# Softmax without the division: undivided probabilities, and weighted values multiplied by reciprocal sums that are spread over channels through memory

## The chip, the core and the metric

The kernel runs on one core of one Trainium2 chip. The metric is the device time of one execution in microseconds, the median over several runs. Names of engines: PE multiplies matrices (PEld are its weight loads), DVE is VectorE, ACT is ScalarE, POOL is GpSimd, SP is the engine that here only issues transfers (DMAs). PSUM is the memory into which PE writes, in 8 banks of 128 x 512 numbers.

## The reference, cut

Two layers over x of shape (8, 512, 256), all in 32-bit floats. Layer 1 (the code's L0) is attention with 16 heads of 64 channels, rotary embeddings and a causal mask, with a quantised linear map beside it; layer 2 (L1) is a masked softmax mixing with a small gated network beside it. The change touches layer 1's attention alone:

```python
xn = layernorm(x)
q, k = rope(xn @ Wq + bq), rope(xn @ Wk + bk)          # 16 heads of 64
v = xn @ Wv + bv
scores = einsum('bnqd,bnkd->bnqk', q, k) / 8           # causal: later keys get -1e9
attn = softmax(scores)                                  # exp(s - max) / sum
attended = einsum('bnqk,bnkd->bnqd', attn, v)           # concatenated over the heads
x = x + attended @ Wo + bo + quantised_linear(xn)
```

## The kernel before

**Units of work.** A step `at` of layer 1 is half of one batch element: 8 of its 16 heads, as four pairs j = 0..3. There are 16 steps, 0 to 15 (`last`); the prediction calls a step a "head" for short ("head 8" is the step at = 8). A step's queries are cut into 16 blocks of 32; block i has scores against its first 32(i+1) keys only. Partition j*32+q of a score tile holds query q of a block for pair j; the second axis e tells the two heads of a pair apart.

**A step, by function.**
- `project_qk(2*at + half, which)` multiplies on PE (tile `pq`, L428), evicts on ACT with a bias (`l`, L434), and sends four DMAs that swap 32-row blocks into a tile `y` (L436). `turn_own` (DVE, `h`, L446) and `turn_other` (DVE `y`, L446, then the sum `h + y` on POOL, L461) apply the rotation. `l` and `y` have two buffers each.
- `scores(at, run)` (PE, `sc`, L509) fills banks for one of five runs of blocks, `soften(at, run)` subtracts the maximum on DVE (L537) and takes the exponential on ACT with the row sums `sm` (L541).
- `divide(at, run)` takes reciprocals of the sums on DVE (L552) and multiplies every block of probabilities by them, on POOL (L560) or, in two places of step 0, on ACT (L558).
- `turn(at, run)` transposes the probabilities in 32 x 32 blocks on DVE (L580), as PE needs keys on the partitions.
- `project_v` and `load_v` bring v, through memory, into the tile `vr` (L472 to L489). `weigh(at)` multiplies it with the turned probabilities (PE, `av`, L597). `keep_weighed(at)` evicts the four results on ACT, adding v's bias as a bias per partition (L611).
- `finish(at)` is `output_product` (PE with `Wo`, `pw`, L390) and `add_output` (DVE, L399) into `x1s[b]`.

**The order** is written out by hand: instructions go to each engine's queue in program order and every engine runs its own queue in order, waiting on semaphores. In the loop over `at`, step at's scores are interleaved with `weigh(at - 1)`, the projections of steps at + 1 and at + 2, and `finish(at - 1)`:

```python
scores(at, 0)
turn(at - 1, 4)
soften(at, 0)
weigh(at - 1)
keep_weighed(at - 1)
turn_qk(2 * at + 2, 1)
load_v(at)
divide(at, 0)
turn_qk(2 * at + 3, 1)
```

Even steps also fetch x of the batch element (`fetch(b)`, 512 KB, L376). Even steps 4 to 12 also turn the next element's input by way of memory (`turn_x`: DVE `xs` L325, a DMA to `xnf` L329, four DMAs to `xnT` L188), which the projection at the end of the same step reads. `add_biases(b)` adds `bo` and another bias to `x1s[b]` on POOL. After step 15 layer 2 follows; its first pieces are already mixed into steps 14 and 15.

Of the kernel before, what the change touches and what calls it, by code (L numbers as in the profile page):

```python
# [8 lines left out]
F32 = mybir.dt.float32  # L9
BF16 = mybir.dt.bfloat16  # L10
I8 = mybir.dt.int8
AF = mybir.ActivationFunctionType
ALU = mybir.AluOpType
# [3 lines left out]
P = 128  # L17
B, S, D = 8, 512, 256
# [11 lines left out]
Q = 32  # L30
# [1 line left out]

UNITS = ((15,), (14, 0), (13, 1), (12, 2), (11, 3), (10, 4), (9, 5), (8, 6), (7,))
RUNS = (UNITS[0:2], UNITS[2:4], UNITS[4:6], UNITS[6:8], UNITS[8:9])
PLACE = {i: n for n, i in enumerate(i for us in UNITS for i in us)}


BIAS = 2 * S
# [6 lines left out]
def two_layers(  # L45
# [14 lines left out]
    def bank(name):  # L60
        return ps.tile([P, S], F32, tag="b", name=name)
# [198 lines left out]
    with ExitStack() as c0:  # L260
# [11 lines left out]
        def line(name):  # L272
            return work.tile([P, S], F32, tag="w", name=name, bufs=2)
# [104 lines left out]
        def add_biases(b):  # L378
            for t in range(NT):
                nc.gpsimd.tensor_tensor(x1s[b][:, t, :], x1s[b][:, t, :], bob, ALU.add)  # L380

        products = {}

        def output_product(at, half):
# [131 lines left out]
        def soften(at, run):  # L516

            if at not in sums_of:
                sums_of[at] = [
                    small.tile([P, 2 * len(PLACE)], F32, tag=f"{n}16", name=f"{n}_{at}", bufs=2)  # L520
                    for n in ("nm", "sm", "rs")
                ]
            nm, sm, _ = sums_of[at]
            for us in RUNS[run]:
                if (at, run) == (last, 0):
                    p = qk.tile([P, 2, S], F32, tag="h0", name=f"p_{at}_{us[0]}")
                elif (at, run) == (0, len(RUNS) - 1):
                    p = work.tile([P, 2, S], F32, tag="xnl", name=f"p_{at}_{us[0]}")
                else:
                    p = prob.tile([P, 2, S], F32, tag="p", name=f"p_{at}_{us[0]}")  # L530
                col = 0
                for i in us:
                    n = Q * (i + 1)
                    chances[at, i] = p[:, :, col : col + n]
                    for e, sc in enumerate(scored.pop((at, i))):
                        c = 2 * PLACE[i] + e
                        nc.vector.tensor_tensor_reduce(  # L537
                            p[:, e, col : col + n], sc, cmask[:, S - n :], -1.0 / L**0.5, BIG,
                            ALU.add, ALU.min, nm[:, c : c + 1],
                        )  # L540
                        nc.scalar.activation(  # L541
                            p[:, e, col : col + n], p[:, e, col : col + n], AF.Exp,
                            bias=nm[:, c : c + 1], scale=-1.0, accum_out=sm[:, c : c + 1],
                        )
                    col += n

        def divide(at, run, on_act=False):
            _, sm, rs = sums_of[at]
            for us in RUNS[run]:
                first = 2 * PLACE[us[0]]  # L550
                which = slice(first, first + 2 * len(us))
                nc.vector.reciprocal(rs[:, which], sm[:, which])  # L552
                for i in us:
                    for e in range(2):
                        c = 2 * PLACE[i] + e
                        p = chances[at, i][:, e, :]
                        if on_act and us is RUNS[run][-1]:
                            nc.scalar.activation(p, p, AF.Copy, scale=rs[:, c : c + 1])  # L558
                        else:
                            nc.gpsimd.tensor_scalar(p, p, rs[:, c : c + 1], 1.0, ALU.mult, ALU.mult)  # L560

        def pitch(c):
            return NT * 4 - 4 * c - 1
# [36 lines left out]
            weighed[at] = banks  # L603

        def keep_weighed(at):
            g = at % NH
            for j, av in enumerate(weighed.pop(at)):
                atts[at, j] = attp.tile([P, S], F32, tag="att", name=f"att_{at}_{j}")

                bv = BIAS + 2 * NP + 4 * g + j  # L610
                nc.scalar.activation(atts[at, j], av, AF.Identity, bias=cs[:, bv : bv + 1])  # L611

# [194 lines left out]
        scores(0, 1)  # L809
        project_qk(2, 0)  # L810
        soften(0, 1)
        divide(0, 0)
        turn_other(2, 1)
        turn_own(2, 0)
        greatest_of(1)
        turn(0, 0)
        divide(0, 1, on_act=True)
        turn_other(2, 0)
        project_qk(3, 1)
        load_v(0)  # L820
# [2 lines left out]
        soften(0, 2)  # L823
        transpose_x(1)
        turn_own(3, 1)
        divide(0, 2)
        turn_other(3, 1)
        turn(0, 1)
        scores(0, 3)
# [3 lines left out]
        soften(0, 4)  # L833
        project_v(1, (1,))
        turn_qk(3, 0)
        divide(0, 3, on_act=True)
        divide(0, 4)
        turn(0, 2)
        x_next.append(load_x(2))
        turn(0, 3)  # L840
# [1 line left out]
        for at in range(1, last):  # L842
            b, g = divmod(at, NH)
            two = at + 2 <= last
            if g == 0 and b < B - 1:
                fetch(b)
            scores(at, 0)
            turn(at - 1, 4)
            soften(at, 0)
            if at == last - 3:  # L850
                scale_of_x()
            weigh(at - 1)
            keep_weighed(at - 1)
            if at == 1:
                load_rest()
                load_second()
                fetch(0)
            turn_qk(2 * at + 2, 1)
            load_v(at)
            if at in (last - 3, last - 2):  # L860
                s_ = at - last + 3
                fetch_output(s_, output_tile(f"x1e_{s_}"))
                xnl = fetch_input(s_, work.tile([P, NK * S], F32, tag="xnl", name=f"xnl_{s_}"))
            divide(at, 0)
            turn_qk(2 * at + 3, 1)
            if at == last - 2:
                first_norm = norm(0, xpool.tile([P, NT, D], F32, tag="x", name="yn_0"))
            scores(at, 1)
            soften(at, 1)
            turn(at, 0)  # L870
            if at == 2:
                look_at(2)
            elif at == 4:
                spread_rest()
                spread_second()
            elif g == 1 and 1 <= b < B - 2:
                look_at(b + 2)
            divide(at, 1)
            if at == last - 1:
                first_norm()  # L880
            project(at + 1, 0)
            if at in (last - 3, last - 2):
                round_input(xnl)
            scores(at, 2)
            soften(at, 2)
            turn_qk(2 * at + 2, 0)
            turn(at, 1)
            if at in (last - 3, last - 2):
                xq = work.tile([P, NK * S], BF16, tag="xq", name=f"xq_{s_}")
                clip(xnl, xq)  # L890
            divide(at, 2)
            if at == 2:
                prepare(2)
            elif g == 1 and 1 <= b < B - 2:
                prepare(b + 2)
            if g == 0 and 1 < b < B - 1:
                turn_x(b + 1)
                if b + 2 < B:
                    x_next.append(load_x(b + 2))
            if at == last - 1:  # L900
                turn_qk(2 * at + 3, 0)
            if at == 1:
                nc.gpsimd.tensor_tensor(bob, bob, rw[:, 2, :], ALU.add)
                add_biases(0)
            project_v(at + 1)
            if at == last - 1:
                break
            if at == 2:
                transpose_x(2)
                x_next.append(load_x(3))  # L910
            scores(at, 3)
            soften(at, 3)
            turn_qk(2 * at + 3, 0)
            turn(at, 2)
            divide(at, 3)
            scores(at, 4)
            soften(at, 4)
            if at in (last - 3, last - 2):
                for half in range(2):
                    add_quantised(s_, half, xq, line(f"u_{s_}_{half}"))  # L920
            finish(at - 1)
            turn(at, 3)
            if two:
                project(at + 2, 1)
            divide(at, 4)
            if g == 0 and b < B - 1:
                add_biases(b)
            if at == last - 4:
                greatest()
# [4 lines left out]
        soften(at - 1, 3)  # L934
        nc.sync.dma_start(w2, second.rearrange("j (k p) n -> p j k n", p=P))
        turn(at - 1, 2)
        divide(at - 1, 3)
        scores(at - 1, 4)
        soften(at - 1, 4)
        output_product(at - 2, 0)  # L940
        scores(at, 0)
        soften(at, 0)
        add_output(at - 2, 0)
        divide(at - 1, 4)
        output_product(at - 2, 1)
        turn_input(0, whole("yt_0", S + 1))
        for s in (1, 0):
            mix_before(0, s)
        turn(at - 1, 3)
        turn(at - 1, 4)  # L950
        add_output(at - 2, 1)
        fetch(B - 1)
        divide(at, 0)
        scores(at, 1)
        soften(at, 1)
        weigh(at - 1)
        for s in (1, 0):
            mix_own(0, s)
        stats_1 = statistics(x1s[1], "b1")
        divide(at, 1)  # L960
        keep_weighed(at - 1)
        load_v(at)
        late[2] = fetch_input(2, work.tile([P, NK * S], F32, tag="xnl", name="xnl_2"))
# [3 lines left out]
        soften(at, 2)  # L967
        sides_of(0, first_sides[:, 0, :], first_sides[:, 1, :])
        turn(at, 1)
        divide(at, 2)  # L970
        scores(at, 3)
        soften(at, 3)
        for half in range(2):
            output_product(at - 1, half)
        turn(at, 2)
        divide(at, 3)
        for half in range(2):
            add_output(at - 1, half)
        scores(at, 4)
        soften(at, 4)  # L980
        turn(at, 3)
        divide(at, 4)
        kk = key(0)
        turn(at, 4)
        r = gate(0)
        round_late(2)
        weigh(at)
# [122 lines left out]
```

## Time and profile before

| what | value |
|---|---|
| three runs | 935.48, 935.68, 936.91 us |
| median | 935.68 us |
| profiled execution, first to last instruction (span) | 934.3 us |
| median less span | 1.4 us |
| TensorE clock granted | 1.000 throughout |
| PE busy, by the page | 919.8 us |
| POOL busy | 542.2 us, of which L560 265.4 us |
| DMA traffic | 108.03 MB, mean 116 GB/s |

The profile shows one execution; its own time outside the span is not given, so the median less the span stands for it. Lines of the profile begin with the start and the length in microseconds or with a source line; "idle before" is the time in which the engine had nothing to run just ahead of that piece, and the name after the arrow is what ended it, inferred from semaphores ("issue" where the profile shows nothing).

### The profile page before, as it was taken

How to read it: one execution, taken by the hardware profiler on the slowest of the kernel's cores; microseconds unless marked ns; L12 is line 12 of the kernel's file. 1: busy time of each engine (PE TensorE's matmuls, PEld its weight loads, DVE VectorE, ACT ScalarE, POOL GpSimd, SP SyncE). 2: the span in 40 equal slices, each digit the busy share in tenths (PEclk: the TensorE clock that was granted, in tenths of full speed). 3: DMA queues.
4: the chain of work that ended last, by engine and by line, in shares of the span. 5: the costliest groups of instructions: out<-in, count | busy, mean ns of one | idle time of the engine just before them, and what ended most of it. 6: DMA issues, size and time to landing. Idle time of an engine off the chain costs nothing.

```text
span 934.3 us, 27432 instructions
## 1 busy us (share of the span) xinstructions
PE 919.8 (98%) x10451; PEld 594.7 (64%) x10451; DVE 793.3 (85%) x2441; ACT 528.3 (57%) x1478; POOL 542.2 (58%) x688
## 2 busy tenths in 40 slices
PE   9998999999999999999999999999999999999998
PEld 5446565656566575757565656566657777777776
DVE  4998898898899889988998899999899588888854
ACT  3585564647465646474746556555577444445553
POOL 2576766655665667566665756678667323444311
PEclk9999999999999999999999999999999999999999
DMA  7667354525543464245444635563435133221011
GB/s 213 194 165 213 102 138 130 121 75 132 169 105 97 109 182 132 75 115 172 123 95 114 179 93 145 151 154 97 110 108 127 47 102 79 74 50 48 25 33 34
DMA packets 70290, 108.03 MB, mean 116 GB/s; under 512 B 8592, under 2 KB 49040, under 8 KB 70160
## 3 DMA queue, kind: packets, MB, share of 16 engines
q1 hardware_dynamic: 68288, 104.64, 42.2%
q10 hardware_dynamic: 1872, 1.64, 0.7%
q8 instruction: 83, 1.36, 0.6%
q14 instruction: 47, 0.39, 0.1%
HBM read 41.76 MB, written 28.84 MB: 76 GB/s over the span
## 4 chain that ended last, share of the span: by engine, by line
PE 85%; DVE 6%; DMA 3%; issue 1%; POOL 1%; SPq 1%; ACT 1%; DVEq 0%; ACTq 0%; POOLq 0%
PE pq L428 21%; PE av L597 14%; PE sc L509 11%; PE pw L390 10%; PE pv L472 8%; PE po L756 6%; PE pk L703 3%; PE pg L718 3%; PE pvv L730 3%; DVE t L580 2%; PE c L675 2%; PE trc L743 1%; PE plr L245 1%; DVE p L537 1%; DMA xnl<-xnf 1%
## 5 line engine op out<-in xcount | busy, mean ns | idle before, releaser
L541 ACT ACTIVATE p<-p,nm 128x64 f32<-128x64 f32 (+15 forms) x512 | 260.0, 512 | 123.8 <-DVE nm L537 100.9
L560 POOL TENSOR_SCALAR p<-p,rs 128x512 f32<-128x512 f32 (+4 forms) x504 | 265.4, 547 | 44.6 <-DVE rs L552 42.6
L461 POOL TENSOR_TENSOR h<-h,y 128x1024 f32<-128x1024 f32 x62 | 161.1, 2598 | 181.5 <-DVE y L446 102.2
L537 DVE CUSTOM_DVE_ANT_0 p<-sc,cmask 128x64 f32<-128x64 f32 (+15 forms) x512 | 190.2, 434 | 53.7 <-PE sc L509 53.7
L580 DVE STREAM_TRANSPOSE t<-p 128x256 f32<-128x256 f32 (+3 forms) x640 | 192.2, 367 | 17.9 <-POOL p L560 17.8
L509 PE MATMUL sc<-h,h 64*32 64x512 f32 (+15 forms) x4096 | 138.7, 393 | 1.3 <-POOL h L461 1.2
L597 PE MATMUL av<-t,vr 32*64 32x384 f32 (+15 forms) x4096 | 128.8, 392 | 3.7 <-issue 3.7
L597 PEld LDWEIGHTS av<-t,vr 32*64 32x64 f32 x4096 | 122.8, 131 | 9.2 <-issue 7.9
L509 PEld LDWEIGHTS sc<-h,h 64*32 64x32 f32 x4096 | 78.6, 106 | 78.5 <-issue 58.3
L434 ACT ACTIVATE l<-pq,cs 128x512 f32<-128x512 f32 x128 | 84.7, 683 | 67.6 <-PE pq L428 53.3
L390 PE MATMUL pw<-wo,att 128*128 128x256 f32 x512 | 114.9, 382 | 0.8 <-DVE nm L537 0.8
L446 DVE TENSOR_TENSOR y<-y,cs 128x1024 f32<-128x1024 f32 x64 | 110.6, 1728 | 5.1 <-DMA y<-l 5.1
L428 PE MATMUL pq<-xnT,wq 128*128 128x512 f32 x256 | 114.6, 599 | 0.2 <-ACT xnT L349 0.2
L428 PE MATMUL pq<-xnT,wk 128*128 128x512 f32 x256 | 113.1, 593 | 1.4 <-DVE x L399 1.0
L472 PE MATMUL pv<-wv,xnT 128*128 128x512 f32 x256 | 114.3, 599 | 0.0
L390 PEld LDWEIGHTS pw<-wo,att 128*128 128x128 f32 x512 | 95.9, 190 | 19.5 <-issue 6.1
L541 ACT ACTIVATION_READ_ACCUMULATOR p<-p,nm 128x1 f32 x512 | 97.3, 190 | 0.0
L428 PEld LDWEIGHTS pq<-xnT,wk 128*128 128x128 f32 x256 | 48.3, 190 | 58.2 <-issue 55.4
L472 PEld LDWEIGHTS pv<-wv,xnT 128*128 128x128 f32 x256 | 47.3, 190 | 57.9 <-issue 54.5
L446 DVE TENSOR_TENSOR h<-l,cs 128x1024 f32<-128x1024 f32 x64 | 80.0, 1252 | 4.3 <-ACT l L434 4.3
L428 PEld LDWEIGHTS pq<-xnT,wq 128*128 128x128 f32 x256 | 47.2, 190 | 56.0 <-issue 48.8
L611 ACT ACTIVATE att<-av,cs 128x512 f32<-128x512 f32 x64 | 38.7, 688 | 71.3 <-PE av L597 71.3
(114 smaller groups left out, 940.7 us busy)
## 6 DMA issues: line engine op xcount, KB each, us to landing
y<-l SPq DMA_DIRECT2D x256, 128.0 KB, 2.3
va<-v SPq DMA_DIRECT2D x32, 512.0 KB, 3.1
vr<-va SPq DMA_DIRECT2D x64, 256.0 KB, 5.1
x<-in_x SPq DMA_DIRECT2D x15, 512.0 KB, 5.0
x1f<-x SPq DMA_DIRECT2D x7, 512.0 KB, 3.2
out<-y SPq DMA_DIRECT2D x14, 256.0 KB, 2.2
xnf<-xs SPq DMA_DIRECT2D x5, 512.0 KB, 3.6
xnT<-xnf SPq DMA_DIRECT2D x20, 128.0 KB, 2.8
```

Source lines behind the costliest of these rows:

```text
L390: nc.tensor.matmul(pw[:, j, :], atts[at, p][:, tok], wo[:, 4 * (at % NH) + p, :], start=(p == 0), stop=(p == 3),)
L428: nc.tensor.matmul(pb.rearrange("p (t a r) -> p t a r", a=4, r=Q), w[:, g, k, bass.ts(t, P)], xnT[b][:, k].rearrange("p a (t r) -> p t a r ...
L434: nc.scalar.activation(l[:, t, :], pb, AF.Identity, bias=cs[:, bias : bias + 1])
L446: nc.vector.tensor_tensor(dst, src, table[:, None, :].to_broadcast([P, 2, S]), ALU.mult)
L461: (engine or nc.gpsimd).tensor_tensor(h, h, y, ALU.add)
L472: nc.tensor.matmul(pb.rearrange("p (g n) -> p g n", g=2), xnT[b][:, k, 2 * half + j], wqkv[2][:, 2 * g : 2 * g + 2, k, :], start=(k == 0), ...
L509: nc.tensor.matmul(scored[at, i][e][j * Q : j * Q + Q, :], q[rows, j % 2, bass.ts(i, Q)], k[rows, j % 2, :n], start=True, stop=True,)
L537: nc.vector.tensor_tensor_reduce(p[:, e, col : col + n], sc, cmask[:, S - n :], -1.0 / L**0.5, BIG, ALU.add, ALU.min, nm[:, c : c + 1],)
L541: nc.scalar.activation(p[:, e, col : col + n], p[:, e, col : col + n], AF.Exp, bias=nm[:, c : c + 1], scale=-1.0, accum_out=sm[:, c : c + 1],)
L560: nc.gpsimd.tensor_scalar(p, p, rs[:, c : c + 1], 1.0, ALU.mult, ALU.mult)
L580: nc.vector.transpose(turned[at][c][:, :, at_ : at_ + (n - 1) * pitch(c) + 1 : pitch(c), :], p[:, :, c * P : c * P + n * Q].rearrange("p e ...
L597: nc.tensor.matmul(banks[j][e * L : e * L + L, i * Q :], vs[at][rows, c, m, bass.ts(e, L)], t[c][rows, e, m * pitch(c) + m : m * pitch(c) ...
```

## The change

Probabilities stay undivided: `divide` and its calls are gone. The sums of step at get columns by head and block (e*16 + i). A new function `settle(at)`, called after the last `turn(at, ..)`, takes all reciprocals at once, transposes them on DVE, writes them to memory (16 KB) so that they lie in the order of queries, and reads them back twice, once for each head of the pairs, repeated over the 64 partitions that are that head's channels. `keep_weighed` copies the results of `weigh` on ACT and multiplies them with that tile on POOL (in step 15 two of the four are multiplied on DVE, from PSUM). As v's bias can no longer be added there, `gather_bias` (step 1) and `spread_bias` (step 2) multiply it with `Wo` once and add it to `bob`, the bias that `add_biases` adds; the first `add_biases` moves from step 1 to step 2. A setting of the program's scratch for DMA descriptors is made smaller.

```diff
+        def gather_bias():
+            both = line("bvwo").rearrange("p (j n) -> p j n", j=2)
+            ones = line("ones")[:, :P]
+            nc.gpsimd.memset(ones, 1.0)
+            for p in range(NP):
+                bv = BIAS + 2 * NP + p
+                nc.gpsimd.tensor_scalar(
+                    both[:, min(p, 1), :], wo[:, p, :], cs[:, bv : bv + 1], None, ALU.mult
+                )
+                if p:
+                    nc.gpsimd.tensor_tensor(both[:, 0, :], both[:, 0, :], both[:, 1, :], ALU.add)
+            nc.gpsimd.tensor_tensor(bob, bob, rw[:, 2, :], ALU.add)
+            gathered[0] = ones, both[:, 0, :]
+
+        def spread_bias():
+            pb = bank("bvwo")
+            nc.tensor.matmul(pb[:, :D], *gathered.pop(0), start=True, stop=True)
+            nc.vector.tensor_tensor(bob, pb[:, :D], bob, ALU.add)
...
-                        c = 2 * PLACE[i] + e
+                        c = e * (S // Q) + i
...
-        def divide(at, run, on_act=False):
-            _, sm, rs = sums_of[at]
-            for us in RUNS[run]:
-                first = 2 * PLACE[us[0]]
-                which = slice(first, first + 2 * len(us))
-                nc.vector.reciprocal(rs[:, which], sm[:, which])
-                for i in us:
-                    for e in range(2):
-                        c = 2 * PLACE[i] + e
-                        p = chances[at, i][:, e, :]
-                        if on_act and us is RUNS[run][-1]:
-                            nc.scalar.activation(p, p, AF.Copy, scale=rs[:, c : c + 1])
-                        else:
-                            nc.gpsimd.tensor_scalar(p, p, rs[:, c : c + 1], 1.0, ALU.mult, ALU.mult)
+        def settle(at):
+            sm = sums_of.pop(at)[1]
+            rs = small.tile([P, Q], F32, tag="rs16", name=f"rs_{at}", bufs=2)
+            turned_ = small.tile([P, Q], F32, tag="rt16", name=f"rt_{at}", bufs=2)
+            nc.vector.reciprocal(rs, sm)
+            nc.vector.transpose(turned_, rs)
+            there = away.tile([4, 2, S], F32, tag="rs", name=f"rsf_{at}")
+            nc.sync.dma_start(there.rearrange("j e (i q) -> (j e i) q", q=Q), turned_)
+            shares[at] = work.tile([P, 4, S], F32, tag="share", name=f"share_{at}")
+            for e in range(2):
+                nc.sync.dma_start(
+                    shares[at][e * L : e * L + L], there[:, e, :][None].to_broadcast([L, 4, S])
+                )
...
-                bv = BIAS + 2 * NP + 4 * g + j
-                nc.scalar.activation(atts[at, j], av, AF.Identity, bias=cs[:, bv : bv + 1])
+                if at == last and j % 2:
+                    nc.vector.tensor_tensor(atts[at, j], av, shares[at][:, j, :], ALU.mult)
+                else:
+                    nc.scalar.copy(atts[at, j], av)
+                    nc.gpsimd.tensor_tensor(atts[at, j], atts[at, j], shares[at][:, j, :], ALU.mult)
...
             scores(at, 0)
             turn(at - 1, 4)
+            settle(at - 1)
             soften(at, 0)
...
-            divide(at, 0)
             turn_qk(2 * at + 3, 1)
...
             if at == 1:
-                nc.gpsimd.tensor_tensor(bob, bob, rw[:, 2, :], ALU.add)
+                gather_bias()
+            elif at == 2:
+                spread_bias()
                 add_biases(0)
...
-    nc = bacc.Bacc("TRN2", target_bir_lowering=False, num_devices=1)
+    nc = bacc.Bacc(
+        "TRN2", target_bir_lowering=False, num_devices=1, dynamic_dma_scratch_size=1024
+    )
```

The other calls of `divide` (those of step 0, of the loop and of the end written out for steps 14 and 15) are deleted in the same way; in that end `settle(at - 1)` follows `turn(at - 1, 4)`, and `settle(at)` follows the last `turn(at, 4)`.

## The prediction

> **What bounds the kernel now.** I read the engine shares first, then PE's own timeline for its gaps, then the rows of the work that the change touches, then one head's transfers in order.
>
> The engine line, the clock line and the chain's summary by engine, from the page:
>
> ```profile
> PE 919.8 (98%) x10451; PEld 594.7 (64%) x10451; DVE 793.3 (85%) x2441; ACT 528.3 (57%) x1478; POOL 542.2 (58%) x688
> PEclk9999999999999999999999999999999999999999
> PE 85%; DVE 6%; DMA 3%; issue 1%; POOL 1%; SPq 1%; ACT 1%; DVEq 0%; ACTq 0%; POOLq 0%
> ```
>
> PE is busy for 98% at full clock. From one `av` to the next (165.17 to 209.41, 255.54 to 299.78) a head takes 44.24 us when PE has no gap, so a lighter POOL or DVE is worth only what they now make PE wait. PE's timeline shows those places (start, length, what, idle before it and its releaser):
>
> ```profile
> 72.52 8.05 PE L597 MATMUL av<-t,vr 32*64 32x512 f32 x256 [2.31 <-issue]
> 217.72 0.32 PE L597 MATMUL av<-t,vr 32*64 32x32 f32 x9 [0.38 <-issue]
> 246.62 7.11 PE L428 MATMUL pq<-xnT,wk 128*128 128x512 f32 x16 [1.05 <-DVE x L399]
> 306.86 1.63 PE L597 MATMUL av<-t,vr 32*64 32x224 f32 x61 [0.44 <-issue]
> 485.39 1.22 PE L597 MATMUL av<-t,vr 32*64 32x288 f32 x37 [0.34 <-issue]
> 693.11 1.93 PE L509 MATMUL sc<-h,h 64*32 64x512 f32 x40 [1.20 <-POOL h L461]
> ```
>
> Only the first and the last come from the divisions. From 694 on PE has no gap, so layer 2 can only lose.
>
> **What the change removes.** The costliest-groups rows (count | busy, mean ns of one | idle before):
>
> ```profile
> L560 POOL TENSOR_SCALAR p<-p,rs 128x512 f32<-128x512 f32 (+4 forms) x504 | 265.4, 547 | 44.6 <-DVE rs L552 42.6
> L461 POOL TENSOR_TENSOR h<-h,y 128x1024 f32<-128x1024 f32 x62 | 161.1, 2598 | 181.5 <-DVE y L446 102.2
> ```
>
> 504 POOL divisions (265.4 us), 8 on ACT and 144 DVE reciprocals of some 0.14 us go. In their place each of 16 heads has four 128x512 products; half of a 128x1024 sum (median 2.366 us) is 1.18 us, so 62 of them are 73 us of POOL, and two go to DVE. POOL loses some 190 us, and none of that counts by itself.
>
> *Ramp.* The last transposes of head 0 waited 0.60 us for POOL and ended at 72.7, which is when `av` could start; ACT's divisions at 47.4 to 49.1 and 66.4 to 68.1 delayed the evictions, and DVE waited 0.51 for an ACT sum and 0.54 for the y transfer that followed from it. Without them DVE reaches the transposes 1.4 us sooner and needs no wait of 0.6: 2.0, plus 0.2 of reciprocals: 2.2 us. Bounds: 1.4 (the waits are replaced by POOL's sums colliding with DVE's products) to 3.6 (the gap of 2.31 and the stretched pieces ahead of it go too).
>
> *Head 15.* POOL's timeline: the sum that the scores need stands behind eight divisions.
>
> ```profile
> 685.09 5.65 POOL L560 TENSOR_SCALAR p<-p,rs 128x384 f32<-128x384 f32 x8 [0.47 <-DVE rs L552]
> 690.70 2.35 POOL L461 TENSOR_TENSOR h<-h,y 128x1024 f32<-128x1024 f32 x1
> ```
>
> Its y was ready at 687.3, so it would end at 689.7, ahead of PE's arrival at 690.85. The scores took 4.12 us (690.85 to 694.97) where other heads need 1.89: 2.2 us. What is late next is DVE, busy 24.97 of 25 us from 700 on: it follows only 0.9 us earlier by `turn(14, 4)`, and drops some 1 us of reciprocals and the 1.06 us wait for POOL at 728.69 after that. I take 1.6, bounds 0.9 and 2.2.
>
> *Elsewhere*, two reciprocals of 0.12 us leave the DVE chains that PE waits for at 144 and 246: 0.4 in all (0 to 1.5). Gains: 2.2 + 1.6 + 0.4 = 4.2 us.
>
> **What it adds and moves.** `gather_bias` is 8 scalings (479 ns at 256 columns), 8 sums (730 ns) and a fill, some 10 us of POOL at head 1, after its divisions have gone; the next sum behind it, `turn_other(5, 0)`, is wanted at 115.9, some 4 us after it would be done: nothing, up to 1 us if not. `spread_bias` is one 256-column product, 0.44 us of PE (7.01 us for 16 in `pw`), right before transposes that idle 1.1 us for DVE at 144: nothing, or 0.44 without that cover. The copy without a bias costs what the eviction of `v` does (578 ns, against 688): a little less ACT, off the path.
>
> `settle` is the real price. Per head (step): two small DVE operations (some 0.25 us, against 9 reciprocals), a 16 KB write to memory and, once that has landed, two reads of 512 KB. On SP they stand behind eight y transfers and `fetch`, and ahead of `load_v`, which waits for `av` anyway. Nearest rows, by DMA issues (KB each, us to landing):
>
> ```profile
> vr<-va SPq DMA_DIRECT2D x64, 256.0 KB, 5.1
> y<-l SPq DMA_DIRECT2D x256, 128.0 KB, 2.3
> xnf<-xnT SPq DMA_DIRECT2D x24, 64.0 KB, 2.2
> q8 instruction: 83, 1.36, 0.6%
> ```
>
> *The late multiplication.* The product waits on POOL for `av`, for ACT's copy and for the reads; behind it on POOL stand both `turn_other(.., 1)`, which today run during `av`. Their sum frees the y buffer that the next projection's transfers write. In head 8 today (SP, DVE, SP, SP):
>
> ```profile
> 404.54 6.09 SPq L436 DMA_DIRECT2D y<-l  x8
> 411.40 1.22 DVE L446 TENSOR_TENSOR y<-y,cs 128x1024 f32<-128x1024 f32 x1
> 416.72 0.35 SPq L329 DMA_DIRECT2D xnf<-xs  x1
> 419.37 2.08 SPq L188 DMA_DIRECT2D xnT<-xnf  x4
> ```
>
> In the changed kernel: SP free at 392.4; write landed 394.6; reads landed 400.4 (four loads of 256 KB, the same 1 MB, took 1.3 to issue and 4.5 to land here); four products to 405.1; the sum to 407.5; y transfers issued from then instead of 404.54, the fourth 1.8 us later and landed 2.5 after that: 411.8. DVE wants it at 411.3: half a microsecond late. Behind DVE's y come the transposes, `xs`, the round trip through memory and `xnT`, for which `pq` waits: at 246 it already does (I read its releaser as that transfer, issued until 243.8), at 514 too (0.35 us), in head 8 there is 0.7 us to spare. Only heads 4, 6, 8, 10 and 12 have this chain. With their own SP times (free 2.0 to 3.4 us after `av` starts) I get 0.4 us in all. Bounds: 0, if the reads land 1 us sooner; 6.2 us, if 2 us later.
>
> *PE's instructions.* q8 moves 83 packets, 1.36 MB: 65 bytes for each of PE's 20,902 records, so it is PE's code, some 250 records a packet. `av` has 512 records in 8 us, a packet every 4 us. The stalls at 217, 306 and 485 stand in heads whose `fetch` had 512 KB moving in the 3 us before. DMA from 213.5 to 216.5, with the packet in it:
>
> ```profile
> GB/s 0 14 68 150 177 287 341 382 369 341 369 410 396 355 369 423 410 341 382 451 205 205 150 96 287 14 0 0 0 0 0 0 0 0 0 0 0 0 0 0
> q1 hardware_dynamic: 504, 0.50, 48.1%
> q8 instruction: 1, 0.02, 2.1%
> ```
>
> Heads without `fetch` have no such gap. The change puts 1 MB under every `av`, from some 4.6 to 9.5 us after its start. I take ten heads at 0.45 us, 4.5 us (the nearest rows are 0.34 to 0.44; the scores behind `av(0)` took 1.0 us too long with more traffic). Bounds: 0 and 15 x 0.95 = 14. The Trainium skill, in "Runtime: NRT & Kernel Launch", section "Instruction fetch mechanics", says that the sequencer fetches the next 16 KiB while it executes the present one, so that a crossing is mostly hidden. By that rule this term is nothing and the sum 932.1; the three rows speak against it.
>
> *Head 14* has its output product only 5.7 us after `av`; `statistics`' 1.02 us on POOL and four products end about when the fourth is wanted: 0.2 (0 to 2). Head 15 has some 2 us to spare. The write has runs of 128 bytes. The skill's "DMA: Bandwidth & Descriptors", section "Specifications", says that under 512 bytes the engine reads, modifies and writes; no row here shows a write of such runs to memory, and the page gives no time for it.
>
> **Sum.** The profiled span is 934.3 us; the median is 935.68, so 1.4 us lie around it, which nothing here touches. 935.68 - 4.2 + 4.5 + 0.4 + 0.2 = 936.6.
>
> **Rivals.**
> *The code arrives in time* (0.27): traffic of the reads, at half of `fetch`'s rate (1 MB in some 5 us as `vr`, against 512 KB in 1.5), leaves room for the code packets. For: `vr` runs under scores without a gap. Against: the three rows. Then 936.6 - 4.5 = 932, and 931.5 if the 0.6 goes too.
> *The reads land late* (0.2): from 1 us over my 5.8, because all partitions read the same 16 KB, which no row shows apart. At 2 us more the five heads lose 1.6, 0.8, 1.9, 1.0 and 0.9 us: 6.2 for my 0.4, so 942.4. For: no slack at 246 and 514. Against: `vr`, same size and same runs.
> *It does not matter* (0.03): neither gaps nor prices show, 935.7.
>
> **How the numbers follow.** The sum above, all priced terms present, has 0.5; its own range is 933 to 939.5 (4.5 may be 2 to 7). It is likeliest, not sure: its terms are larger than their difference. A measurement of this kernel can tell some 0.2%, 1.9 us, from no change: under 933.8 is faster, over 937.6 slower. Of the forecast 0.10 is faster, 0.20 same, 0.20 slower; of the first rival 0.23 and 0.04; the second is 0.20 slower; the third 0.03 same. Together 0.33, 0.27, 0.40. For 8 in 10 the range reaches from 930.5 to 942.
>
> **What would show it.** Right: `av(0)` without its 2.31, head 15's scores at 1.9 us, PE gaps marked "issue" late in most `av`, SP's y issues released by POOL. Wrong: PE busy as a share unchanged in `av` (then the first rival), gaps at `pq` in even heads of 1 us and more (the second), or a gap in front of `pw` of heads 14 and 15.

## The result, and the profile after

The changed kernel took 984.66 us (median of four runs, 979.66 to 990.88) where the kernel before, on the same chip, took 936.29: a ratio of 1.052, 95% interval 1.047 to 1.057. It is 48 us slower; the prediction had 936.6 and a range to 942. The profiled execution has a span of 979.6 us, 45.3 more than before.

The engine line of the page, its clock line and the chain's summary by engine:

```profile
PE 937.9 (96%) x10453; PEld 598.3 (61%) x10453; DVE 777.8 (79%) x2332; ACT 518.4 (53%) x1468; POOL 363.6 (37%) x262
PEclk9999899999999999999999999989999999999999
PE 67%; DMA 11%; DVE 8%; POOL 5%; SPq 3%; issue 3%; ACT 1%; DVEq 0%; POOLq 0%; ACTq 0%
```

DVE, ACT and POOL all have less to do, POOL by a third. PE has about the same instructions, but is idle for 41.7 us instead of 14.5 (+27.2) and busy for 18.1 us more. Most of the second number is not work: the mean granted clock is 0.984, and 1.6% of 979.6 us is some 15 us. DMA has gone from 3% to 11% of the chain.

What PE waited for (us in total, times, longest):

```profile
PE pq L448 <- DMA xnT<-xnf: 13.4, 4, 3.8
PE sc L529 <- issue: 5.8, 3, 2.7
PE av L615 <- issue: 4.7, 2, 2.6
PE acc L208 <- DVE xq L200: 4.1, 1, 4.1
PE sc L529 <- POOL h L481: 4.0, 2, 3.8
```

In the kernel before, the first was 0.4, "issue" 4.0 in all (2.3 of it the gap ahead of `av(0)`), the last 1.2, and no wait for `xq` was listed. The timeline, at the places that answer to those of before (start, length, what, idle before it; PE, but for the last line, which is POOL's):

```profile
68.68 8.04 PE L615 MATMUL av<-t,vr 32*64 32x512 f32 x256
117.27 3.64 PE L529 MATMUL sc<-h,h 64*32 64x512 f32 x40 [3.76 <-POOL h L481]
252.62 8.80 PE L448 MATMUL pq<-xnT,wk 128*128 128x512 f32 x16 [2.69 <-DMA xnT<-xnf]
726.55 1.63 PE L529 MATMUL sc<-h,h 64*32 64x512 f32 x8
728.39 1.93 PE L529 MATMUL sc<-h,h 64*32 64x512 f32 x40 [0.20 <-POOL h L481]
725.96 2.37 POOL L481 TENSOR_TENSOR h<-h,y 128x1024 f32<-128x1024 f32 x1 [2.60 <-DVE y L466]
```

The first line is a gain that was forecast: `av(0)` starts 3.84 us sooner and without its gap. The next two are new waits, and the pieces behind them are stretched: 3.64 us for 40 matmuls that take 1.93 elsewhere, 8.80 for a projection that takes 7.1. The last three are the scores of step 15. Their listed wait fell from 1.20 to 0.20, but the first eight records now take 1.63 us instead of 1.06, so that the scores take 3.70 us (726.55 to 730.25) where they took 4.12. The sum that they need no longer stands behind divisions on POOL; it waits for DVE's y.

From one `av` to the next, the steps that became longer by over 1 us are 1 (6.7), 2 (1.9), 4 (2.9), 6 (3.3), 8 (5.8), 9 (2.4), 10 (4.4), 12 (6.0), 13 (6.1), 14 (1.1) and 15 (4.1), and what follows is 4.4 longer. Steps 3, 5, 7 and 11 lost at most 0.2, steps 4, 6, 8, 10 and 12 lost 2.9 to 6.0: that points at x's way through memory, which only these five have. Step 8 shows it (SP, POOL, SP, DVE; its `av` starts at 399.94):

```profile
403.40 0.44 SPq L576 DMA_DIRECT2D rsf<-rt  x1
407.19 1.30 SPq L579 DMA_DIRECT2D share<-rsf  x2
408.58 2.19 SPq L509 DMA_DIRECT2D vr<-va  x4
415.70 4.97 POOL L631 TENSOR_TENSOR att<-att,share 128x512 f32<-128x512 f32 x4 [22.76 <-DMA share<-rsf]
423.02 5.71 SPq L456 DMA_DIRECT2D y<-l  x8
427.31 1.23 DVE L466 TENSOR_TENSOR y<-y,cs 128x1024 f32<-128x1024 f32 x1 [3.24 <-DMA y<-l]
```

The write is out at 403.40, but the reads could only be issued at 407.19, and the products on POOL started at 415.70, 8.5 us later. Both sums stand behind them on POOL, the y buffer comes free at about 423, and the y transfers that went out 15.5 us after the start of `av` go out 23.1 us after it. DVE waits 3.24 us for y; behind that y stand the turning of x, its round trip through memory, and `pq`, which starts 3.28 us late at 439.61.

Step 12, whose `av` starts at 591.51, has the same chain, but its wait is listed under `acc`, the quantised map's product (SP, DVE, PE):

```profile
614.74 5.70 SPq L456 DMA_DIRECT2D y<-l  x8
619.67 1.23 DVE L466 TENSOR_TENSOR y<-y,cs 128x1024 f32<-128x1024 f32 x1 [3.88 <-DMA y<-l]
624.75 1.86 PE L208 MATMUL acc<-w8b,xq 128*128 128x256 bf16 x8 [4.14 <-DVE xq L200]
```

Here y goes out 23.2 us after the start of `av`, where it went out 15.4 us after it before; DVE makes `xq` behind that y, without a pause between them.

### The profile page after: what moved, and what is told of

The parts are those of the page before. It is cut to its first block, busy times and chain, and to the rows that moved or that the text cites. A ratio compares the mean times of both kernels' runs of the same rounds, so it can differ in the third digit from the quotient of the medians.

```text
span 979.6 us, 26929 instructions
## 1 busy us (share of the span) xinstructions
PE 937.9 (96%) x10453; PEld 598.3 (61%) x10453; DVE 777.8 (79%) x2332; ACT 518.4 (53%) x1468; POOL 363.6 (37%) x262
## 4 chain that ended last, share of the span: by engine, by line
PE 67%; DMA 11%; DVE 8%; POOL 5%; SPq 3%; issue 3%; ACT 1%; DVEq 0%; POOLq 0%; ACTq 0%
PE pq L448 16%; PE av L615 10%; PE sc L529 8%; PE pw L410 7%; PE pv L492 6%; PE po L776 6%; DVE t L598 3%; PE pvv L750 3%; DMA share<-rsf 3%; PE pk L723 3%; PE pg L738 3%; POOL att L631 3%; POOL h L481 2%; DMA y<-l 2%; SPq L456 2%
## 5 line engine op out<-in xcount | busy, mean ns | idle before, releaser
L481 POOL TENSOR_TENSOR h<-h,y 128x1024 f32<-128x1024 f32 x62 | 152.9, 2477 | 157.8 <-DVE y L466 157.8
L631 POOL TENSOR_TENSOR att<-att,share 128x512 f32<-128x512 f32 x62 | 77.4, 1282 | 282.4 <-DMA share<-rsf 208.3
L529 PE MATMUL sc<-h,h 64*32 64x512 f32 (+15 forms) x4096 | 142.7, 396 | 9.8 <-issue 5.8
L615 PE MATMUL av<-t,vr 32*64 32x32 f32 (+15 forms) x4096 | 131.9, 395 | 6.1 <-issue 4.7
L448 PE MATMUL pq<-xnT,wk 128*128 128x512 f32 x256 | 118.0, 614 | 13.4 <-DMA xnT<-xnf 13.4
L448 PE MATMUL pq<-xnT,wq 128*128 128x512 f32 x256 | 117.4, 611 | 0.2 <-ACT xnT L348 0.2
L466 DVE TENSOR_TENSOR y<-y,cs 128x1024 f32<-128x1024 f32 x64 | 79.4, 1241 | 30.7 <-DMA y<-l 27.4
L466 DVE TENSOR_TENSOR h<-l,cs 128x1024 f32<-128x1024 f32 x64 | 87.4, 1367 | 4.3 <-ACT l L454 4.3
L630 ACT COPY att<-av 128x512 f32<-128x512 f32 x62 | 32.0, 599 | 78.0 <-PE av L615 78.0
```

The source lines that it names most:

```text
L448: nc.tensor.matmul(pb.rearrange("p (t a r) -> p t a r", a=4, r=Q), w[:, g, k, bass.ts(t, P)], xnT[b][:, k].rearrange("p a (t r) -> p t a r ...
L466: nc.vector.tensor_tensor(dst, src, table[:, None, :].to_broadcast([P, 2, S]), ALU.mult)
L481: (engine or nc.gpsimd).tensor_tensor(h, h, y, ALU.add)
L529: nc.tensor.matmul(scored[at, i][e][j * Q : j * Q + Q, :], q[rows, j % 2, bass.ts(i, Q)], k[rows, j % 2, :n], start=True, stop=True,)
L615: nc.tensor.matmul(banks[j][e * L : e * L + L, i * Q :], vs[at][rows, c, m, bass.ts(e, L)], t[c][rows, e, m * pitch(c) + m : m * pitch(c) ...
L631: nc.gpsimd.tensor_tensor(atts[at, j], atts[at, j], shares[at][:, j, :], ALU.mult)
```

## The experiments

Times are medians, each against the kernel before on the same chip (936.5 to 937.6). The theory after the comparison: the transfers cost it all, partly by making the products late on POOL, partly by themselves. Rivals: the products' mere place, or `gather_bias`, whose 16 us stand ahead of the sum in step 1.

### No transfers at all

```diff
 def settle(at):
-    there = away.tile(...); nc.sync.dma_start(there..., turned_)
-    shares[at] = work.tile(...); two dma_starts into it
+    shares[at] = one_share[0]      # filled with 1.0 once
```

> The changed kernel without settle's write and reads: the products take a tile of ones that is filled once (so the output is undivided). Theory (the reads cost, by their wait and by their traffic): pq's gaps for xnT and the gaps called issue in av and the scores are gone; what stays is gather_bias at step 1 with some 6.7 us, less some 4 us of gains: 936 to 941 us. Rival (the cost is the products on POOL or the reciprocals on DVE, not the transfers): 975 us or more, gaps at pq as they are.

Measured: 935.02, ratio 0.998 (0.996 to 1.000), a little below what was expected. Every instruction of the change is there but the writes and reads, and the 48 us are gone: they are the transfers' price. What the new arithmetic gains, it spends: in the profile `pq` still waits once for `xnT`, 2.1 us, and the scores of step 2 wait 2.8 us for a sum behind `gather_bias`.

### The products behind the sums

```diff
+    # in the loop, behind turn_qk(2 * at + 3, 1):
+    for j in range(4): share_out(at - 1, j)     # the product on POOL
```

> The changed kernel, steps 1 to 14: ACT's copies stay, POOL's four products are issued behind both turn_other(.., 1) sums instead of ahead of them; every transfer stays. Theory of two causes (late sums make y, xs and xnT late in even steps; the reads' traffic holds up PE's code packets): pq's 13.4 us of gaps and the 4.1 at acc go with the slow clock behind them, the issue gaps of 1.5 to 2.8 us stay: 957 to 967 us. Rival (one cause, the traffic, which also makes y late): less than 5 us better, 979 us or more.

Measured: 958.51, ratio 1.025 (1.022 to 1.029). So 26 of the 48 us hang on the products' place in POOL's queue. Its profiled execution, its shortest at 946.3, has no gap before `pq` for `xnT` left. Its runs spread up to 963.9, and what its longer ones waited for isn't seen.

### The reads behind the loads of v

On top of that, `read_shares(at - 1)` was moved behind `load_v(at)` on SP.

> As e2_sums_first, and in steps 1 to 14 the two reads are issued on SP behind load_v instead of ahead of it, so that they move under the projections, where PE takes few instructions per microsecond. Theory: the issue gaps in steps 1 to 13 go as well; gather_bias's step and the ends written out for steps 14 and 15 keep their cost: 941 to 950 us. Rival (any 1 MB more per step holds PE's code up, wherever it moves): as e2_sums_first. Second rival (the reads now stand ahead of the y transfers and make these late): pq's gaps come back, 965 us or more.

Measured: 989.03, ratio 1.056 (1.053 to 1.058): as bad as the change itself. The reads now lie under the y transfers, whose median landing goes from 2.3 to 3.4 us, and PE waits 7.9 us in front of `av` for DVE's transposes. This later place on the queue is no better than the first.

### `gather_bias` at the end of step 1

> The changed kernel with gather_bias at the end of step 1 instead of ahead of project_v, behind turn_other(5, 0). Theory: the wait of 3.76 us of the scores for POOL and the 1.31 us ahead of pv at step 1 go, with the slow clock after them: 5 to 8 us better than the changed kernel. Rival (step 1 is slow for its heavy transfers): within 2 us of the changed kernel.

Measured: 974.58, ratio 1.040 (1.037 to 1.043), 10 us better than the change. The gap of 3.76 is gone, another of 4.8 in front of `pxt` in step 2 has come, and the four waits for `xnT` are still 12.4 us.

### The transfers alone, in the kernel before

```diff
 # before.py, behind turn(at - 1, 4)
+settle(at - 1)     # writes rs, reads 2 x 512 KB into a tile that nobody uses
```

> The kernel before, divisions and all, plus the write of 16 KB and the two reads of 512 KB at the places of the changed kernel; nothing reads what they bring. Two causes (the transfers by themselves cost some 23 us, as the runs with and without them in the order 'sums first' differ): 953 to 965, with PE gaps marked issue and gaps where x or y comes late, no product on POOL that could wait. All by the wait on POOL: 936 to 941, no new gap.

Measured: 952.65, ratio 1.014 (1.011 to 1.018), just under the lower edge. The transfers cost 16 us with nothing waiting for them. "Issue" waits are 9.7 us in front of `av` and `sc` where before had 3.7 in front of `av`, with the same 83 packets of 16 KB on q8. Of the 9.7, 4.8 stand inside a run of matmuls, where before had 1.2. The rest stands at the start of `av(0)` (2.32, before 2.31) and of `av(1)` (2.47, before 0.19), where DVE's last transposes end just before `av`: the list calls such a wait "issue" too.

### A quarter of the volume

```diff
-shares[at] = work.tile([P, 4, S], ...); reads of there[:, e, :]
+shares[at] = work.tile([P, 1, S], ...); reads of there[:1, e, :]
```

> The changed kernel, but only the sums of one of the four pairs of heads are read back (two reads of 128 KB a step) and used for all four: the products of three pairs take the wrong sums, the work on every engine stays. If the volume makes the reads late and crowds the other transfers: reads landed some 5 us after issue, 940 to 950, gaps in front of pq under 1 us. If it is the way itself (write, wait, read, on the queue), whatever the size: 965 to 982, gaps of 3 us and more in front of pq in even steps as now.

Measured: 940.15, ratio 1.003 (1.001 to 1.005). The same 16 writes and 32 reads, waits and products, in the same order, but 256 KB instead of 1 MB, and 44 of the 48 us are gone. The reads land in 3.1 us at the median instead of 6.7; PE waits 1.9 us for `xnT` and 0.7 for "issue" in all. It is the volume, not the way through memory as such.

### Pauses in the kernel before

PE's clock had to be told apart from its waits. A matmul of one column was set behind the projection of q in 14 steps, waiting for a transfer just issued:

```diff
 project(at + 1, 0)
+nc.tensor.matmul(bank(...)[:, :1], y[:, 0, :P], y[:, 0, :1], ...)   # y of evicted[2 * at + 3, 0]
```

> The kernel before with a single matmul of one column after the projection of q in steps 1 to 14, which waits for the y transfer just issued: 14 pauses of PE of some 3.2 us, 45 us, no other work. If a pause costs only itself, and other waits hide in it: 970 to 981, granted clock 1.00. If the clock falls for a while behind each pause, as behind the gaps of the changed kernel (7 windows of 25 us at 0.86 to 0.94, some 15 us in all): 985 to 1005, mean clock 0.97 to 0.985.

Measured: 1046.4, ratio 1.115 (1.112 to 1.118), more than either theory expected, because the pauses were 5.2 to 8.9 us and not 3.2. One pause by windows of 2 us (busy time of PE, PEld, DVE, ACT, POOL, then the clock, DMA share, GB/s):

```profile
410.00:412.00 2.00, 0.00 (x0) 0.00 (x0) 0.00 (x0) 0.00 (x0) 2.00 (x5) 0.98 0.96 217
412.00:414.00 2.00, 0.00 (x0) 0.00 (x0) 0.00 (x0) 0.00 (x0) 0.95 (x3) 0.50 0.62 141
414.00:416.00 2.00, 1.89 (x26) 1.07 (x34) 0.00 (x0) 0.00 (x0) 0.00 (x0) 0.50 0.03 8
416.00:418.00 2.00, 2.00 (x56) 0.96 (x40) 1.35 (x7) 0.69 (x3) 0.00 (x0) 0.50 0.00 0
418.00:420.00 2.00, 2.00 (x12) 1.04 (x5) 1.76 (x11) 2.00 (x10) 0.00 (x0) 0.81 0.00 0
420.00:422.00 2.00, 2.00 (x6) 0.80 (x6) 2.00 (x2) 1.82 (x7) 0.00 (x0) 1.00 0.00 0
```

PE stood from 408.9 to 414.1. The clock fell to 0.50 at about 412 and came back at about 418.6, so 4.5 us of work ran at half speed. The profiled span grew by 109.3 us: 76.4 of idle time and 32.9 of longer busy time, 7.8 us a pause for 5.5 us of standing still. Nothing else was changed, and the same matmuls without a pause leave the clock at 0.999 (next run), so the fall of the clock follows from the stop.

Two more lengths were tried, by what the matmul waits for: ACT's `l`, and the first of the two y transfers.

> As the run with the pauses, but the single matmul waits for ACT's eviction l in place of the y transfer: 14 pauses of some 1 us. If the clock only falls behind longer idle time: 945 to 955, clock 1.00. If every stop of PE costs clock: above 965, clock under 0.985.

> As the run with the pauses, but the matmul waits for the first of the two y transfers, issued some 3.5 us sooner: 14 pauses of some 1.8 us. If a stop of under 2 us leaves the clock alone: 955 to 966, clock 1.00 (each pause costs its own length). If shorter stops pull it down too: 968 to 985, clock 0.97 to 0.99.

The first made hardly any pause (PE was idle for 15.1 us in all instead of 14.5; 938.23): it shows only that the matmul itself costs nothing, and says nothing of the clock. The second made pauses of 2.4 to 4.2 us, with one of 6.0, not the 1.8 expected, and took 1001.0. Seven of its 14 pauses were followed by half clock, seven not, and length doesn't sort them: 2.69 us was and another 2.69 was not, 3.28 was not (the last section shows what does). The loss came in pieces: 3.4 us at half clock five times, 6.8 twice.

### Only step 0 undivided

> Only step 0 goes undivided (its products on POOL behind both sums, with the bias behind them); all others as before. If the ramp's gain of 3.8 us is kept and one step's transfers cost no more than 1 us: 932 to 934. If the 1 MB under av of step 0 costs what it costs a step on average in the changed kernel (some 3 us): 935 to 937.

Measured: 940.98, ratio 1.004 (1.002 to 1.005), above both ranges. `av(0)` starts at 69.31 instead of 72.52, so the ramp's gain comes from step 0's divisions. But four products and four additions of the bias keep POOL for 12.6 us in step 1, and what stands behind them on POOL runs 3.3 us late: a sum, for which PE waits 1.33 us, and then step 1's divisions. DVE's last transposes wait for these divisions, 1.06 us as in the kernel before, but start at 120.71 instead of 117.45; `av(1)` starts right behind, at 121.25 instead of 118.00, after a wait of 4.03 us that the list calls "issue". More than the gain is spent one step later.

### The loads of v moved away from the reads

```diff
-    load_v(at)                 # ahead of turn_qk(2 * at + 3, 1)
...
     project(at + 1, 0)
+    load_v(at)
```

Together with the products behind the sums, and then by itself:

> The kernel with the sums ahead of the products, and the four loads of vr (1 MB) moved on SP behind the y transfers of the next projection, so that the reads of the sums are alone under av. If the two megabytes side by side make the remaining 22 us: reads landed some 5 us after issue, 944 to 952. If the reads crowd out PE's code by themselves, or vr only collides later: 954 to 962.

> The changed kernel with nothing but the loads of vr moved behind the y transfers of the next projection; the products stay ahead of both sums. The prediction took 5.8 us for the reads by themselves and 0.4 us for the late products in all. If its chain was right and only the landing wrong: reads landed after some 5.7 us, gaps in front of pq in even steps under 1.5 us, 946 to 955. If the products ahead of the sums are late anyway: 965 to 978.

With the sums first: 945.69, ratio 1.009 (1.006 to 1.012). By itself: 990.98, ratio 1.058 (1.055 to 1.061), no better than the change, and not what the prediction's chain gives. Even alone on the queue the reads took 7.5 (step 9) and 7.9 us (step 8) from first issue to the first product, and in step 8 the write before them 3.9, behind `fetch`; `vr` now lies under x's round trip, whose `xnT` loads go out 5.0 us behind `xnf` instead of 2.65.

### Other ways to spread the sums

32 KB read back to one partition in 32, and one DVE `stream_shuffle`; or two rows and two `partition_broadcast`s on POOL (both with `gather_bias` in two halves):

> The changed kernel with 32 KB read back in place of 1 MB a step (one partition of each group of 32), spread over the partitions by one DVE stream_shuffle of 128x2048 behind turn(at, 0), the four products on POOL behind it; gather_bias in two halves, one behind each projection's sums of step 1. If the volume was the price: no gap in front of pq above 1 us, 929 to 935. If DVE's 2 us or more a step (its share was 79 to 85%) take the place of the transfers: 938 to 955, gaps released by DVE t, h or y.

> As the run with the shuffle, but POOL, idle for 60%, spreads the two rows (two partition_broadcasts of 2048 elements a step) in place of DVE. If the shuffle only failed because DVE had no time: 928 to 935, under the kernel before, gaps at most those of before. If POOL's custom operations hold DVE up or make the sums late: 938 to 955, with gaps released by POOL h or by DVE.

DVE: 946.13, ratio 1.010 (1.009 to 1.012). The shuffle takes 2.49 us a step, DVE goes to 842.9 us (89%), and six waits of 0.4 to 2.4 us on DVE take the place of the transfers. POOL: 1101.63, ratio 1.177. Waits on POOL in its profile:

```profile
POOL att L590 <- issue: 107.4, 15, 8.2
POOL share L587 <- issue: 66.9, 11, 6.6
```

The two broadcasts take 2.3 and 2.5 us, but POOL stands some 6 us ahead of them and 7 us ahead of the ordinary product behind them, waiting for nothing that the profile shows, and PE waits 68.2 us in front of `pw`.

### Is it the same 16 KB for all partitions?

> As the run with only vr moved, but the reads take 1 MB of different rows (a copy of x, of which the write overwrites 16 KB) in place of the same 16 KB for 64 partitions each: the products are wrong but for the first rows. If reading the same rows over and over makes the reads slow: landed some 5.7 us after the first issue instead of 7.5, gaps in front of pq in even steps 1.5 us shorter, 975 to 984. If 1 MB takes this long from any place: landing and time as there, 987 to 994.

Measured: 990.43, ratio 1.056 (1.054 to 1.058), like its twin. The median landing of one read fell from 6.3 to 5.3 us, but the products start 7.2 and 7.6 us after the first issue in steps 8 and 9, where they started 7.9 and 7.5. So this rival, which the prediction gave as the reason for late reads, explains at most 0.7 us of one step and none of the time. Why two reads of 512 KB take this long where four loads of 256 KB took 5.8 stays open.

### The order of step 14 alone

```diff
-divide(at, 2)              # ahead of prepare, turn_x, turn_qk(2 * at + 3, 0)
+# in step 14: behind turn_qk(2 * at + 3, 0)
```

> The kernel before, with one line moved: in step 14 the divisions of the third run go behind the sum that the scores of head 15 need. If the eight divisions were what held these scores up: the gap of 1.20 us in front of them goes, 934.5 to 936. If DVE or the transpose behind the divisions is late in its place: 936.5 to 938.

Measured: 937.35 against 937.58, ratio 1.000 (0.999 to 1.002). PE's timeline:

```profile
690.53 1.96 PE L509 MATMUL sc<-h,h 64*32 64x512 f32 x48
700.92 8.61 PE L597 MATMUL av<-t,vr 32*64 32x512 f32 x256 [1.86 <-DVE t L580]
```

The scores' gap is gone, and `av` starts 0.62 us sooner (701.54 before), but now waits 1.86 us for DVE: what was next in line took it.

### The scalings in two operations, and all three costs eased

```diff
-both[:, min(p, 1), :], wo[:, p, :], cs[:, bv : bv + 1], None, ALU.mult
+both[:, min(p, 1), :], wo[:, p, :], cs[:, bv : bv + 1], 1.0, ALU.mult, ALU.mult
```

> The changed kernel, but the 8 scalings of gather_bias are written with a second multiplication by 1.0, as the divisions of the kernel before were. If the form made them dear (0.92 us each against 0.48 in the divisions' row): gather_bias 12 to 12.5 us in place of 16, the gap of 3.76 at 113.5 at most 1 us, no half clock behind it, 976 to 981. If a scaling costs 0.92 here in any form (the weights' tile, the sums between): gap and time as before, 982 to 988.

> Sums ahead of the products, vr behind the y transfers, and the scalings in two operations: the change with its three costs eased, the volume kept. From 945.7 less the gap of 1.45 that the sum h left: 942 to 945, still slower than the kernel before by 5 to 8 us, for PE's code under the reads. If more than the volume is gone: under 938.

The first: 976.75, ratio 1.043 (1.042 to 1.045), 8 us better than the change for a multiplication by one. Most scalings take 0.48 us instead of 0.92, `gather_bias` 12.8 us instead of 16, and the gap of 3.76 is 0.83. The second: 941.49, ratio 1.005 (1.003 to 1.006), the best kernel with the full volume, still 5 us slower than before. What PE waits for in it:

```profile
PE av L615 <- issue: 5.9, 5, 3.2
PE sc L529 <- issue: 3.5, 2, 3.3
PE pq L448 <- DMA xnT<-xnf: 0.5, 1, 0.5
```

What is left is "issue". No version beat the kernel before by more than can be measured.

## Why the prediction was wrong

**Ramp, 2.2 us: right, and small.** `av(0)` came 3.84 us sooner, just over the upper bound of 3.6, and the gap of 2.31 went too. With step 0 alone undivided, 3.2 us of it came.

**Elsewhere, 0.4 us: swallowed.** The 1.1 us of waits around 145 in front of `pxt` are gone, but the wait of 1.05 at 246 gave way to the one of 2.69 for `xnT`.

**Head 15, 1.6 us: the divisions did hold the scores, but the gain did not come.** With only the order changed the scores took 1.96 us and `av` then waited 1.86 for DVE: what was next in line took the gain. In the changed kernel DVE was late already at the sum: its y ended just before the sum began at 725.96, 0.6 us ahead of PE's arrival at 726.55, where the kernel before had y ready at 687.3, 3.5 us ahead. So the scores took 3.70 us instead of 4.12, not the 1.9 forecast. The prediction named DVE as next and still booked the 1.6.

**`gather_bias`, 0 to 1 us: a wrong price.** The step took the scaling's 479 ns from the divisions' row. That row is of two multiplications in one instruction; the new scaling has one, and took 0.92 us. 16 us in place of 10 made the sum 3.8 us late, and half clock ran from 116.2 to 123.0 behind it: step 1 lost 6.7 us.

**The late multiplication, 0.4 us (0 to 6.2): the step that failed.** The chain was the right one, link by link: SP, the write, the reads, POOL, y, DVE, x's round trip, `pq`. The durations were not. The write was taken from the rows of other small transfers (2.2 us): the reads followed it after 3.8 us in step 8, where `fetch` had gone out just before it, and after 3.3 in step 9, where it had not. The reads were taken from `vr`, as if `vr` itself were not issued right behind them: 8.5 us for 5.8, of which the runs without `vr` beside them account for about 1 and leave 7.2 to 7.9. Together with sums of 2.83 instead of 2.35 us each, DVE's y came 27.4 us after the start of `av`, where the forecast had its transfer landed after 22.8 and the kernel before had it after 22.4: 5.0 us later than before, where the chain had 0.7 to spare. Four steps lost 13.4 us of waiting in front of `pq` and step 12 lost 4.1 in front of `acc`; four of the five fell to half clock behind it, 1.7 us each. That makes some 24 us, near the 26 that the run with the products behind the sums won. The rival *The reads land late* was this case, but it went only to 2 us more and stopped at 942.4; the upper bound of the term was set by nothing in the trace.

**PE's instructions, 4.5 us: inside its bounds, but half the size.** Without the gap ahead of `av(0)`, which belongs to the ramp, the "issue" waits went from 1.7 to 10.5 us: not ten of 0.45, but five of 1.5 to 2.8, two of them with half clock behind them. That more traffic makes them and not the change's code is shown by three runs with the same 83 packets. Inside runs of matmuls, where before had 1.2 us of such waits, they came to 4.8 with the transfers alone, 0.7 with a quarter of the volume, 0.5 with none. That it is the code's packets in particular was only argued, from where the gaps stand. The rule weighed against it, of the Trainium skill, "Runtime: NRT & Kernel Launch", section "Instruction fetch mechanics", that a crossing is mostly hidden, fits the runs with little traffic; if these waits are the code's, it does not fit those with much.

**Head 14, 0.2 us: not seen.** No wait of `pw` for POOL is listed. What PE waited for in `av(14)` was DVE's transposes, 1.5 us, and "issue", 2.6 us.

**No term for the clock.** Before showed 1.00 throughout, so every loss was priced at the length of the wait. In the changed kernel the clock took up to some 15 of 45.3 us.

**The signs that were named** came but for one: no gap ahead of `av(0)`, "issue" gaps (in five steps, not in most), SP's y transfers held back by POOL, and, for the rival, gaps of 2.7 to 3.8 us in front of `pq` in even steps. Head 15's scores at 1.9 us did not come.

## What to carry to other kernels

Before pricing a transfer by a row of the trace, ask what else lies on the queue and the engines in the microseconds in which the new one runs, its own neighbours included; a row from a quiet place is a lower bound. Where PE is busy for 98%, a megabyte a step that nobody waits for still has a price (16 us here), and what stands ahead of a sum on an in-order queue is priced by who waits for that sum, several links on. A stop of PE costs its length and, from some 2 us on, often another 1.7 or 3.4 us in clock.

## What was not expected of the hardware

**The clock behind a stop.** In the changed kernel gaps of 2.03, 2.69 and 2.75 us were followed by half clock for 3.4 us or twice that, while one of 2.62 and one of 3.76 (in front of `pq` in step 6) were not; gaps up to 1.6 never were. Each period costs 1.7 us of work. The Trainium skill, "TensorE: Matmul & The Clock Gate", section "What's actually happening", tells of a free-running window of 3.4 us, which fits both the length of the periods and that a gap's place matters beside its length. The rule in its section "HAM oscillation — how this bites in real kernels", no idle gaps over some 3.4 us, was not strict enough here: 2.0 us was enough in one case.

What sorts the stops is their place. All changes of the clock in a trace lie on one grid of 3.413 us: in the changed kernel half clock begins at 116.2, 252.8, 440.5, 536.1, 624.8, 655.5 and 781.8, always a whole number of steps apart. Cut along that grid from 20 us on, the changed kernel and the two runs with longer pauses have 28 windows at full clock in which PE was busy for 1.38 us or less, and half clock followed every one; it followed none of 784 with 1.51 us or more, and of two in between it followed the one with 1.50 and not the one with 1.40. The pause of 3.28 us lay across two windows, with 1.58 and 1.96 us busy; one of 2.80 lay mostly in one, with 0.61. The edge is not sharp: in the other runs, half clock also followed four windows with 1.6 to 1.9 us.

**POOL's scaling with one operation** is dearer than with two: 0.92 against 0.48 us for 128x256.

**POOL between a broadcast and ordinary operations** stood idle for some 6 to 7 us each way in the one kernel that had broadcasts; why is not shown.
